# Where a recurrent kernel's bias enters PSUM, and three smaller moves around it

## The chip, the core and the metric

The kernel runs on one NeuronCore of a Trainium2 chip. The time is device microseconds of one launch; smaller is better. The core has five engines that run beside each other and meet only at semaphores: TensorE (PE, matrix products into PSUM), VectorE (DVE), ScalarE (ACT), GpSimd (POOL) and SyncE (SP, which here only issues DMAs; ACT issues a few too). Each engine works through its own instructions in order.

## The reference

The input is `x` of 16 batches, 512 time steps and 512 features, and one condition vector of 512 per batch. Four layers follow one another, each added to its input:

```python
x = x + L0(x, cond)   # levels of sums and differences, gated: comes to x * (1 + gate)
x = x + L1(x, cond)   # h = tanh(x_t @ Wx + b + h @ Wh), h0 = cond, over 512 steps
x = x + L2(x, cond)   # gated recurrence: sigmoids, cumulative sums along time
x = x + L3(x, cond)   # x @ (base + A_b B_b): A, B of rank 8, made from cond by a small network
```

All of it is float32. The bias of L1, `b`, is what this case is about: it is a vector of 512 that is added to each step's input before the tanh.

## The kernel before

**Start (lines 126 to 264).** DMAs bring the small vectors and weights in. `turned_layer` computes L0's gate from the condition in two layers of 16 matrix products (`ps_hq`, then `ps_g`); DVE turns and adds, ACT takes the sigmoid, and the gate plus 2 becomes `g2`. `gated` multiplies a block of the input by it (`x1`, four DVE instructions). Beside this the layer norm of the condition goes through four small PE transposes into `aeT`. The L1 bias is loaded by ACT's DMA queue into three rows of `rest`, split by POOL into three bfloat16 pieces whose sum is the float32 value, and kept in three rows of `bias_rows`. Last, the table `b2a` (8 numbers for each of 512 rows of L3's first factor) is loaded into `b2a_raw` by ACT's queue (line 229), transposed by PE (line 231) and copied by DVE (line 232) to `b2a_sb`. Only the last stage reads it.

**Recurrence (lines 446 to 525).** 64 blocks of `T = 8` steps. The order of PE, ACT, DVE and SP is written by hand here: instructions stand in each engine's queue as the Python code emits them. All batches go together. A PSUM tile `pre` of three banks holds the sums of one block; two generations of it (of bufs=2) are in use, one for the block that runs (`pre`) and one for the next (`nxt`). `PAIRS` and `PLACE` say that a place of 128 columns serves two steps: bank 0 has the pairs (0, 5) and (2, 7), bank 1 (4, 1), bank 2 (6, 3). In each step `s` of block `n`:

- PE adds 16 products of the last state with `wh_sb` (`accumulate`, line 465), waiting chunk by chunk for `h_out`;
- PE adds two of the 16 input pieces of the next block (`inputs`, line 475), each four products with `wx_sb`; when a piece is the first of its bank, the bias goes in before it: four bfloat16 products of `ones_rows` with `bias_rows` (line 354), which with `start=True` also open the bank. That falls on step 0 (bank 0, 256 columns), step 2 (bank 1, 128 columns) and step 6 (bank 2, 128 columns);
- from block 1 to 16, in steps 4 to 7, PE adds four products of L3's small network (`factor_part`; in block 0 the first layer of it);
- from block 16 on, in each step, PE computes a quarter of a unit of L2's gates for the first 128 times, eight products of 256 columns (`early_gate`, line 382). Three units make a group of 12 steps: f, i, candidate. Their sigmoids and the DVE work on them are laid into later steps by `later` and `do_jobs`;
- ACT takes four tanhs of 128x32 (line 491) and DVE four transposes of 128x32 into `h_out` (line 492), on which the next step's products wait; DVE then adds the states to `x2` or gates input of block n+2; then come the jobs of the step.

In block 0 the pieces of block 0 itself stand in steps 0 to 2 too, beside those of block 1. At the end of block 0 `finish_first` takes a Gelu on ACT, which needs a load of its table.

**Last stage (lines 527 to 629).** For each batch, four chunks `j` of L2 (`gate_unit`: 12 products of 384 columns on PE, two sigmoids on ACT, some 9 us of DVE, two adds on POOL, giving `x3[:, j]`). After chunk 2 `make_layer` forms L3's matrix: four products into PSUM tiles (two of tag `pl`, two of the tag `po` that the output also uses), and four DVE additions of `base_sb` spread among the next chunk's DVE work. `last_layer` of a batch stands after chunk 1 of the next one, in the last batch after chunk 3: 4 x 4 products of 512 columns into `po`, ACT copies, DMAs out. The last batch's matrix is written over `base_sb`.

Of the kernel before, what the change touches and what calls it, by code (L numbers as in the profile page):

```python
# [35 lines left out]
P = 128  # L36
# [4 lines left out]
T = 8  # L41
# [21 lines left out]
def kernel(  # L63
# [55 lines left out]


# [8 lines left out]
    nc.gpsimd.memset(hT3, 0.0)  # L129
    for h in h_out[G - 2 : T - 1]:  # L130
        nc.gpsimd.memset(h, 0.0)

    bias_rows = rw.tile([P, D], BF16)
    ones_rows = rw.tile([P, BP], BF16)
    thirds = [slice(i * BP, i * BP + 1) for i in range(3)]
    nc.gpsimd.memset(bias_rows, 0.0)
    nc.gpsimd.memset(ones_rows, 0.0)
    for rows in thirds:
        nc.gpsimd.memset(ones_rows[rows, :], 1.0)
# [36 lines left out]
    with tc.tile_pool(name="pre", bufs=1, side="right") as pre, tc.tile_pool(  # L176
# [36 lines left out]
        rest = pre.tile([P, D], F32)  # L213
        piece = pre.tile([P, D], BF16)
        nc.gpsimd.memset(rest, 0.0)
        for rows in thirds:
            nc.scalar.dma_start(
                out=rest[rows, :].rearrange("p (k n) -> p k n", k=KC),
                in_=l1b.rearrange("(o k) n -> o k n", o=1),
            )  # L220
        for i, rows in enumerate(thirds):
            nc.gpsimd.tensor_copy(piece, rest)
            nc.gpsimd.tensor_copy(bias_rows[rows, :], piece[rows, :])
            if i < 2:
                nc.gpsimd.tensor_tensor(rest, rest, piece, ALU.subtract)

        b2a_raw = pre.tile([P, KC, BP], F32)
        nc.gpsimd.memset(b2a_raw, 0.0)
        nc.scalar.dma_start(out=b2a_raw[:, :, :R], in_=b2a)
        ps = ps_pre.tile([P, P], F32, tag="ae", name="b2a_turned")  # L230
        nc.tensor.transpose(ps, b2a_raw.rearrange("p k r -> p (k r)"), ident)
        nc.vector.tensor_copy(b2a_sb, ps)
# [112 lines left out]
    def inputs(n, i, pre):  # L345

        g, k = divmod(i, KC)
        bank, place = PLACE[g]
        if k == 0 and place == 0:

            n_place = sum(b == bank for b, _ in PLACE)
            for j in range(KC):
                row = tile_columns(bias_rows, j).unsqueeze(1).to_broadcast([P, n_place, KC, BP])
                nc.tensor.matmul(  # L354
                    pre[bank][j * BP : (j + 1) * BP, :n_place, :],
                    ones_rows,
                    row,
                    start=True,
                    stop=False,
                    skip_group_check=True,  # L360
                )
# [80 lines left out]
    def fresh(n):  # L442
        return [ps_r.tile([P, G, P], F32, tag=f"pre{i}", name=f"pre_{n}_{i}") for i in range(NBANK)]
# [4 lines left out]
    pre = fresh(0)  # L448
# [3 lines left out]
    for n in range(NBLK):  # L452
        if n + 1 < NBLK:
            nxt = fresh(n + 1)
# [5 lines left out]
        for s in range(T):  # L460
# [12 lines left out]
            if n + 1 < NBLK:  # L473
                for i in range(2 * s, 2 * s + 2):
                    inputs(n + 1, i, nxt)
# [31 lines left out]
            do_jobs(q)  # L507
        if n == 0:
            finish_first(loaded)
        elif loaded:  # L510
            store_factor(n - 1, loaded)
# [10 lines left out]
        pre, loaded = nxt, coming  # L522
# [92 lines left out]
    for b in range(B):  # L615
# [72 lines left out]
```

## Time and profile before

| what | us |
|---|---|
| median of 3 runs (1676.74 to 1680.77) | 1678.63 |
| the profiled execution | 1677.59 |
| its span, first to last instruction | 1675.8 |
| first tanh of the recurrence starts | 25.45 |
| first tanh of block 1 starts | 41.95 |
| first products of the last stage | 925.64 |
| last product of PE ends | 1672.16 |

How busy the engines are in some stretches of that span, in us of busy time:

| stretch | length | PE | DVE | ACT | POOL |
|---|---|---|---|---|---|
| 56.80 to 255.00, blocks 2 to 15 and some | 198.20 | 192.17 | 97.60 | 56.55 | 0.00 |
| 270.00 to 910.00, blocks 17 to 61 and some | 640.00 | 638.00 | 371.47 | 192.58 | 0.00 |
| 925.60 to 1580.00, batches 0 to 13 of the last stage | 654.40 | 654.17 | 554.44 | 97.26 | 183.17 |
| 1635.10 to 1641.44 | 6.34 | 0.00 | 6.34 | 0.00 | 0.56 |

The lines of the trace are read as: start, duration, engine, line of the kernel, operation, what it writes and reads, shape, count, and in brackets the idle time of the engine before it and who ended it. A matrix product's duration includes its way through the array: 16 products of 128 columns in float32, which the trace counts as 32 instructions, follow each other 0.03 us apart although each lasts 0.27 us. So PE counts as busy while it waits for a short time; the start times tell more.

### The profile page before, as it was taken

What the parts mean: (1) busy time and instruction counts of PE and PEld (TensorE: products, weight loads), DVE (VectorE), ACT (ScalarE), POOL (GpSimd) and SP (SyncE); (2) the same over time, 40 slices, a digit from 0 to 9 for tenths busy, and PEclk for the clock granted to TensorE, in tenths of its full rate; (3) what the DMA queues carried; (4) which work ended last, traced back from release to release, by engine and by line L of the source; (5) the groups of instructions that cost most, each with busy time, mean ns of one, the idle gap of its engine ahead of it and who ended that gap; (6) DMA issues with size and microseconds to landing.
All of it is one profiled execution on the core that took longest, in us unless ns stands there. A gap on an engine that the chain in (4) does not pass through costs nothing.

```text
span 1675.8 us, 71396 instructions
## 1 busy us (share of the span) xinstructions
PE 1638.2 (98%) x31205; PEld 1196.9 (71%) x31205; DVE 1126.2 (67%) x3557; ACT 381.6 (23%) x2315; POOL 213.4 (13%) x223
## 2 busy tenths in 40 slices
PE   6999999999999999999999999999999999999997
PEld 5888889898898888999998555555555555555553
DVE  3444545555555555555555888889888888888894
ACT  2222232323323322333323111111111111111111
POOL 2000000000000000000000222232232323222231
PEclk9999999999999999999999999999999999999998
DMA  5344331111111111111110011110101111111101
GB/s 190 104 142 151 117 96 31 36 36 36 34 35 36 36 36 36 36 36 36 36 36 17 24 40 40 38 37 22 39 33 38 40 37 40 37 40 38 40 15 50
DMA packets 100239, 83.61 MB, mean 50 GB/s; under 512 B 10307, under 2 KB 78403, under 8 KB 99926
## 3 DMA queue, kind: packets, MB, share of 16 engines
q1 hardware_dynamic: 99392, 79.02, 15.2%
q8 instruction: 244, 4.00, 1.0%
q14 instruction: 69, 0.57, 0.1%
q10 hardware_dynamic: 534, 0.02, 0.0%
HBM read 53.32 MB, written 25.69 MB: 47 GB/s over the span
## 4 chain that ended last, share of the span: by engine, by line
PE 89%; DVE 6%; issue 2%; DMA 1%; ACT 1%; POOL 0%; ACTq 0%; SPq 0%; DVEq 0%; POOLq 0%
PE pre L336 40%; PE po L607 12%; PE pg L382 10%; PE pf L541 8%; PE pi L541 8%; PE pc L541 8%; DVE s L558 2%; PE pf L308 1%; PE pl L597 1%; DVE s L566 1%; PE pre L354 1%; DVE h_out L492 1%; DVE s L570 1%; ACT a L491 1%; DMA b2a_raw<-in_b2a_dram 0%
## 5 line engine op out<-in xcount | busy, mean ns | idle before, releaser
L336 PE MATMUL pre<-wh_sb,h_out 128*32 128x128 f32 x16384 | 563.1, 274 | 7.4 <-DVE h_out L492 1.4
L336 PEld LDWEIGHTS pre<-wh_sb,h_out 128*32 128x32 f32 x16384 | 462.1, 110 | 97.0 <-DVE h_out L492 71.1
L492 DVE STREAM_TRANSPOSE h_out<-a 128x32 f32<-128x32 f32 x2048 | 262.0, 185 | 364.1 <-ACT a L491 363.5
L491 ACT ACTIVATE a<-pre 128x32 f32<-128x32 f32 x2048 | 238.3, 202 | 627.0 <-PE pre L336 626.8
L336 PE MATMUL pre<-wx_sb,x 128*32 128x128 f32 x8192 | 336.9, 274 | 2.0 <-issue 1.4
L336 PEld LDWEIGHTS pre<-wx_sb,x 128*32 128x32 f32 x8192 | 245.4, 110 | 5.5 <-issue 4.6
L607 PE MATMUL po<-layer,x 128*128 128x512 f32 x480 | 211.5, 599 | 6.3 <-DVE base_sb L600 6.3
L541 PE MATMUL pf<-x,wf_sb 128*128 128x384 f32 x512 | 177.3, 489 | 1.0 <-DVE x L497 1.0
L607 PEld LDWEIGHTS po<-layer,x 128*128 128x128 f32 x480 | 92.2, 192 | 120.2 <-issue 108.8
L541 PE MATMUL pi<-x,wi_sb 128*128 128x384 f32 x512 | 175.6, 486 | 0.0
L541 PE MATMUL pc<-x,wc_sb 128*128 128x384 f32 x512 | 175.6, 486 | 0.0
L558 DVE RECIPROCAL s<-s 128x384 f32<-128x384 f32 x64 | 163.4, 2553 | 2.2
L541 PEld LDWEIGHTS pf<-x,wf_sb 128*128 128x128 f32 x512 | 95.9, 190 | 79.9 <-issue 18.1
L541 PEld LDWEIGHTS pc<-x,wc_sb 128*128 128x128 f32 x512 | 97.3, 190 | 67.8
L541 PEld LDWEIGHTS pi<-x,wi_sb 128*128 128x128 f32 x512 | 97.3, 190 | 67.8
L575 POOL TENSOR_TENSOR s<-s,f 128x512 f32<-128x512 f32 x64 | 87.5, 1367 | 388.8 <-DVE s L570 376.2
L497 DVE TENSOR_TENSOR x<-x,h_out 128x128 f32<-128x128 f32 x256 | 101.1, 395 | 37.5 <-PE pg L382 13.8
L530 POOL MEMSET zero<- 128x1 f32 x1 | 0.1, 100 | 913.7 <-DMA early<-ei 913.7
L557 DVE SCALAR_TENSOR_TENSOR s<-f,i 128x384 f32<-128x384 f32 x64 | 36.6, 572 | 101.7 <-ACT i L556 101.7
L556 ACT ACTIVATE f<-pf,vec_sb 128x384 f32<-128x384 f32 x64 | 37.3, 583 | 276.1 <-POOL s L575 117.3
L611 ACT COPY osb<-po 128x512 f32<-128x512 f32 x64 | 37.5, 586 | 273.7 <-PE po L607 159.5
L382 PE MATMUL pg<-x,wc_sb 128*32 128x256 f32 x1024 | 84.0, 379 | 0.0
(88 smaller groups left out, 1317.7 us busy)
## 6 DMA issues: line engine op xcount, KB each, us to landing
xb<-in_xT_dram SPq DMA_DIRECT2D x64, 256.0 KB
w<-in_l3w_dram SPq DMA_DIRECT2D x64, 256.0 KB
out_dram<-osb SPq DMA_DIRECT2D x64, 256.0 KB
early<-ef SPq DMA_DIRECT2D x32, 128.0 KB
early<-ei SPq DMA_DIRECT2D x32, 128.0 KB
f<-early SPq DMA_DIRECT2D x64, 64.0 KB
i<-early SPq DMA_DIRECT2D x64, 64.0 KB
w_sb<-in_w1T_dram SPq DMA_DIRECT2D x1, 1024.0 KB
```

The lines of the kernel that those rows point to most:

```text
L336: nc.tensor.matmul(pre[PLACE[g][0]][j * BP : (j + 1) * BP, PLACE[g][1], :], lhsT, tile_columns(w, j), start=False, stop=False, skip_group_ ...
L382: nc.tensor.matmul(ps[c * BP : (c + 1) * BP, :, :], w[:, k, j * P + c * BP : j * P + (c + 1) * BP], x2[:, k, pair, :TE], start=(k == 0), s ...
L491: nc.scalar.activation(a[:, at], pre[bank][:, place, at], AF.Tanh)
L492: nc.vector.transpose(turned[:, c, :], a[:, at])
L497: nc.vector.tensor_tensor(x2[:, :, :, at].rearrange("p k b t -> p k t b"), xs[n][:, :, t0 // 2, :, :], turned.rearrange("p k (t b) -> p k ...
L541: nc.tensor.matmul(p[:, TE:], w_sb[:, k, j * P : (j + 1) * P], x2[:, k, b, TE:], start=(k == 0), stop=(k == KC - 1),)
L556: nc.scalar.activation(gate[:, new], p[:, new], AF.Sigmoid, bias=col(bias, j))
L557: nc.vector.scalar_tensor_tensor(s[:, new], f[:, new], EPS, i[:, new], ALU.add, ALU.add)
L558: nc.vector.reciprocal(s[:, new], s[:, new])
L575: nc.gpsimd.tensor_tensor(s, s, f, ALU.add)
L607: nc.tensor.matmul(po, x3[:, k, at], layer[:, k, :], start=(k == 0), stop=(k == KC - 1))
L611: nc.scalar.copy(osb, po)
```

## The change

- **Bias.** `bias_sb`, a float32 tile that holds the bias broadcast over the partitions, is loaded by four DMAs of ACT's queue. A new `begin(n, i)` allots one bank of block `n` and lets ACT copy the bias into it; the products of `inputs` add to that. In the banks' first two generations (blocks 0 and 1) PE first writes zeros with 32 products of a zero tile and `ident`, with `start=True` on the first of each bank and quarter. The products of line 354, `bias_rows`, `ones_rows` and POOL's splitting go.
- **When.** Bank 0 of block n+2 is begun at the end of step 7 of block n, bank 1 of block n+1 after step 0, bank 2 after step 2, each after the jobs of the step. Blocks 0 and 1 are begun ahead of the loop.
- **b2a.** Its memset and DMA stay at the start (the DMA now directly behind those of the bias on ACT's queue); its PE transpose and DVE copy go to the end of block 2.
- **Inputs in block 0.** Block 1's 16 pieces, two in each step before, stand in steps 3 to 7 as 3, 4, 3, 3, 3.
- **Last batch.** `make_layer` of the last batch stands after chunk 1 instead of 2.

In the built program the layer norm's transposes also stand ahead of `ps_hq` on PE, and its DVE work ahead of `z_hq`. The issue of `b2a_raw` on ACT's queue waits for the first of the four bias DMAs, and the table load and square root of the layer norm stand behind it.

```diff
-    bias_rows = rw.tile([P, D], BF16)
-    ones_rows = rw.tile([P, BP], BF16)
...
+    bias_sb = rw.tile([P, KC, BP], F32)
...
+        for j in range(KC):
             nc.scalar.dma_start(
-                out=rest[rows, :].rearrange("p (k n) -> p k n", k=KC),
-                in_=l1b.rearrange("(o k) n -> o k n", o=1),
+                out=bias_sb[j * BP : (j + 1) * BP],
+                in_=l1b[:, j * BP : (j + 1) * BP]
+                .rearrange("(o c) f -> o c f", o=1)
+                .to_broadcast([BP, KC, BP]),
             )
-        for i, rows in enumerate(thirds):
-            nc.gpsimd.tensor_copy(piece, rest)
-            nc.gpsimd.tensor_copy(bias_rows[rows, :], piece[rows, :])
-            if i < 2:
-                nc.gpsimd.tensor_tensor(rest, rest, piece, ALU.subtract)
...
         nc.scalar.dma_start(out=b2a_raw[:, :, :R], in_=b2a)
-        ps = ps_pre.tile([P, P], F32, tag="ae", name="b2a_turned")
-        nc.tensor.transpose(ps, b2a_raw.rearrange("p k r -> p (k r)"), ident)
-        nc.vector.tensor_copy(b2a_sb, ps)
...
     def inputs(n, i, pre):
         g, k = divmod(i, KC)
-        bank, place = PLACE[g]
-        if k == 0 and place == 0:
-            n_place = sum(b == bank for b, _ in PLACE)
-            for j in range(KC):
-                row = tile_columns(bias_rows, j).unsqueeze(1).to_broadcast([P, n_place, KC, BP])
-                nc.tensor.matmul(
-                    pre[bank][j * BP : (j + 1) * BP, :n_place, :],
-                    ones_rows,
-                    row,
-                    start=True,
-                    stop=False,
-                    skip_group_check=True,
-                )
...
+    def begin(n, i):
+        bank = ps_r.tile([P, G, P], F32, tag=f"pre{i}", name=f"pre_{n}_{i}")
+        n_place = sum(b == i for b, _ in PLACE)
+        if n < 2:
+            for j in range(KC):
+                for place in range(n_place):
+                    nc.tensor.matmul(
+                        bank[j * BP : (j + 1) * BP, place, :],
+                        h0[:, 0, :BP],
+                        ident,
+                        start=(place == 0),
...
+        nc.scalar.copy(
+            bank[:, :n_place, :],
+            bias_sb.rearrange("p c f -> p (c f)").unsqueeze(1).to_broadcast([P, n_place, P]),
+        )
+        return bank
+    SHARE = ((0, 0), (0, 0), (0, 0), (0, 3), (3, 7), (7, 10), (10, 13), (13, 16))
+    BEGINS = {T - 1: 0, 0: 1, 2: 2}
...
-    pre = fresh(0)
+    pre = [begin(0, i) for i in range(NBANK)]
+    nxt = [begin(1, i) for i in range(NBANK)]
...
-                for i in range(2 * s, 2 * s + 2):
+                for i in range(*((2 * s, 2 * s + 2) if n else SHARE[s])):
                     inputs(n + 1, i, nxt)
...
             do_jobs(q)
+            if s in BEGINS:
+                if s < T - 1 and 0 < n < NBLK - 1:
+                    nxt.append(begin(n + 1, BEGINS[s]))
+                elif s == T - 1 and n + 2 < NBLK:
+                    ahead.append(begin(n + 2, BEGINS[s]))
...
+        if n == 2:
+            turned = ps_q.tile([P, P], F32, tag="pg", name="b2a_turned")
+            nc.tensor.transpose(turned, b2a_raw.rearrange("p k r -> p (k r)"), ident)
+            nc.vector.tensor_copy(b2a_sb, turned)
...
-            if j == 2:
+            if j == (1 if end else 2):
```

More of the change, by code (lines that the diff above doesn't have):

```diff
@@ L118 @@
     wh_sb = rw.tile([P, KC, D], F32)
+    b2a_raw = rw.tile([P, KC, BP], F32)
     h_out = [rw.tile([P, KC, HP], F32, name=f"h_out_{i}") for i in range(2 + G)]
@@ L129 @@
     nc.gpsimd.memset(hT3, 0.0)
+    nc.gpsimd.memset(b2a_raw, 0.0)
     for h in h_out[G - 2 : T - 1]:
         nc.gpsimd.memset(h, 0.0)
-    bias_rows = rw.tile([P, D], BF16)
-    ones_rows = rw.tile([P, BP], BF16)
[L135 to L139, printed above, removed]
+    bias_sb = rw.tile([P, KC, BP], F32)
     def load_x(n, pool=xpool):
@@ L211 @@
             )
[L213 to L216, printed above, removed]
+        for j in range(KC):
             nc.scalar.dma_start(
-                out=rest[rows, :].rearrange("p (k n) -> p k n", k=KC),
-                in_=l1b.rearrange("(o k) n -> o k n", o=1),
-            )
-        for i, rows in enumerate(thirds):
-            nc.gpsimd.tensor_copy(piece, rest)
-            nc.gpsimd.tensor_copy(bias_rows[rows, :], piece[rows, :])
-            if i < 2:
-                nc.gpsimd.tensor_tensor(rest, rest, piece, ALU.subtract)
-        b2a_raw = pre.tile([P, KC, BP], F32)
-        nc.gpsimd.memset(b2a_raw, 0.0)
+                out=bias_sb[j * BP : (j + 1) * BP],
+                in_=l1b[:, j * BP : (j + 1) * BP]
+                .rearrange("(o c) f -> o c f", o=1)
+                .to_broadcast([BP, KC, BP]),
+            )
         nc.scalar.dma_start(out=b2a_raw[:, :, :R], in_=b2a)
-        ps = ps_pre.tile([P, P], F32, tag="ae", name="b2a_turned")
-        nc.tensor.transpose(ps, b2a_raw.rearrange("p k r -> p (k r)"), ident)
-        nc.vector.tensor_copy(b2a_sb, ps)
         def turned_layer(src, w_sb, which, name):
@@ L440, in do_jobs @@
             job()
-    def fresh(n):
-        return [ps_r.tile([P, G, P], F32, tag=f"pre{i}", name=f"pre_{n}_{i}") for i in range(NBANK)]
+    def begin(n, i):
[9 more added lines that the diff above has]
+                        start=(place == 0),
+                        stop=False,
+                        skip_group_check=True,
+                    )
+        nc.scalar.copy(
+            bank[:, :n_place, :],
+            bias_sb.rearrange("p c f -> p (c f)").unsqueeze(1).to_broadcast([P, n_place, P]),
+        )
+        return bank
+    SHARE = ((0, 0), (0, 0), (0, 0), (0, 3), (3, 7), (7, 10), (10, 13), (13, 16))
+    BEGINS = {T - 1: 0, 0: 1, 2: 2}
     E = mybir.EngineType
     rnn.enter_context(tc.manual_schedule(engines={E.PE, E.Activation, E.DVE, E.SP}))
-    pre = fresh(0)
+    pre = [begin(0, i) for i in range(NBANK)]
+    nxt = [begin(1, i) for i in range(NBANK)]
     for i in range(KC):
@@ L452 @@
     for n in range(NBLK):
-        if n + 1 < NBLK:
-            nxt = fresh(n + 1)
+        ahead = []
         if n + 2 < NBLK:
@@ L521 @@
                 nc.vector.scalar_tensor_tensor(diag, ident, 2.0, diag, ALU.mult, ALU.add)
-        pre, loaded = nxt, coming
+        if n == 2:
+            turned = ps_q.tile([P, P], F32, tag="pg", name="b2a_turned")
+            nc.tensor.transpose(turned, b2a_raw.rearrange("p k r -> p (k r)"), ident)
+            nc.vector.tensor_copy(b2a_sb, turned)
+        pre, nxt, loaded = nxt, ahead, coming
     for q in sorted(jobs):
```

## The prediction

> **What bounds the kernel now.** I read the page's busy times and chain of waits first, to see which engine carries the end, and then the timeline at four places where the change acts.
>
> ```profile
> PE 1638.2 (98%) x31205; PEld 1196.9 (71%) x31205; DVE 1126.2 (67%) x3557; ACT 381.6 (23%) x2315; POOL 213.4 (13%) x223
> ...
> PE pre L336 40%; PE po L607 12%; PE pg L382 10%; PE pf L541 8%; PE pi L541 8%; PE pc L541 8%; DVE s L558 2%; PE pf L308 1%; PE pl L597 1%; DVE s L566 1%; PE pre L354 1%; DVE h_out L492 1%; DVE s L570 1%; ACT a L491 1%; DMA b2a_raw<-in_b2a_dram 0%
> ```
>
> PE is busy 98% and nearly all of the chain is PE. The products of the bias (L354) hold 1%. Whether removing them pays must be read step by step, since a PE that waits inside a running product counts as busy. First, steps of block 1 (timeline; the tanh marks a step):
>
> ```profile
> 45.17 0.24 PE L354 MATMUL pre<-bias_rows,ones_rows 128*32 128x128 bf16 x4
> ...
> 45.42 0.47 ACT L491 ACTIVATE a<-pre 128x32 f32<-128x32 f32 x4 [1.05 <-PE pre L336]
> ...
> 47.06 0.47 ACT L491 ACTIVATE a<-pre 128x32 f32<-128x32 f32 x4 [1.18 <-PE pre L336]
> ...
> 48.71 0.47 ACT L491 ACTIVATE a<-pre 128x32 f32<-128x32 f32 x4 [1.18 <-PE pre L336]
> ```
>
> From tanh to tanh 1.64 and 1.65 us, the first with four bias products in it, the second without. Here the loop tanh, transpose, 16 products, tanh sets the step, and PE has room: the products of the state take 0.89 (45.92 to 46.81) and the pieces 0.45. A step of block 33 with the gates' products in it:
>
> ```profile
> 484.64 0.29 PE L354 MATMUL pre<-bias_rows,ones_rows 128*32 128x256 bf16 x4
> 484.89 0.47 ACT L491 ACTIVATE a<-pre 128x32 f32<-128x32 f32 x4 [1.28 <-PE pre L336]
> ...
> 486.75 0.47 ACT L491 ACTIVATE a<-pre 128x32 f32<-128x32 f32 x4 [1.39 <-PE pre L336]
> ...
> 488.49 0.47 ACT L491 ACTIVATE a<-pre 128x32 f32<-128x32 f32 x4 [0.92 <-PE pre L336]
> ```
>
> With the 256-column bias the step takes 1.86, the next, without, 1.74, the same as for many steps of this region; the 128-column ones give 1.79 to 1.80. Here PE is the bound: state 0.87, pieces 0.43, gates 0.44. Third, the start:
>
> ```profile
> 10.48 1.72 DVE L249 TENSOR_TENSOR z_hq<-z_hq,vec_sb 128x128 f32<-128x128 f32 x1
> ...
> 12.30 0.62 ACTq L229 DMA_DIRECT2D b2a_raw<-in_b2a_dram  x1
> ...
> 16.27 0.31 ACT L251 ACTIVATE gate_g<-z_g 128x128 f32<-128x128 f32 x1 [3.73 <-DVE z_g L249]
> ...
> 20.07 0.45 PE L231 MATMUL b2a_turned<-ident,b2a_raw 128*128 128x128 f32 x1 [4.55 <-DMA b2a_raw<-in_b2a_dram]
> 20.56 0.29 DVE L232 COPY b2a_sb<-b2a_turned 128x128 f32<-128x128 f32 x1 [4.33 <-PE b2a_turned L231]
> 20.77 0.18 DVE L258 TENSOR_SCALAR g<-gate_g 128x64 f32<-128x64 f32 x1
> ...
> 21.74 1.93 PE L336 MATMUL pre<-wx_sb,x 128*32 128x128 f32 x32 [0.43 <-DVE x L162]
> ```
>
> PE, DVE and so the first pieces of the recurrence (21.74) stood behind the landing of `b2a_raw` at about 20.0, although the gate was done at 16.58. Fourth, the last batch:
>
> ```profile
> 1632.36 2.74 PE L541 MATMUL pc<-x,wc_sb 128*128 128x384 f32 x8
> ...
> 1640.73 1.26 DVE L600 TENSOR_TENSOR base_sb<-pl,base_sb 128x512 f32<-128x512 f32 x2
> ...
> 1641.44 16.98 PE L607 MATMUL po<-layer,x 128*128 128x512 f32 x32 [6.34 <-DVE base_sb L600]
> ...
> 1652.66 1.27 POOL L576 TENSOR_TENSOR x<-s,x 128x512 f32<-128x512 f32 x1
> ```
>
> PE has nothing to do from 1635.10 to 1641.44: the output of batch 14 needs PSUM tiles that the last two additions to `base_sb` release, and these stand late in DVE's queue. The first 16 products then take 16.98 instead of 13.73, the time of every earlier batch.
>
> **What the Trainium skill says.** "PSUM — Partial Sum Buffer", The four PSUM rules: writes of VectorE and ScalarE neither set nor clear the bits by which a product decides to add or to overwrite. So zeros by PE are needed once for each buffer, and later generations can be seeded by ACT; no run here shows it. "TensorE: Matmul & The Clock Gate", Part 1: PE runs at half rate until it was busy for a window of about 3.4 us, and again after an idle one. The trace agrees: 32 instructions take 1.48 from 21.74 and 0.88 from 27.01, and weight loads take 0.34 instead of 0.19 after the gap at 1635. "SBUF — State Buffer", SBUF: two separate sides: a DVE instruction with two SBUF inputs and a GpSimd one that reads SBUF exclude each other. The trace agrees: the addition to `z_hq` at 10.48 took 1.72, beside POOL's bias work, its twin at 15.94 took 0.29.
>
> **Step 1, the start.** `ps_hq` begins with the landing of w1 at 8.14, as before; the four bias DMAs and the earlier b2a put about a thousand small packets ahead, 0.2 assumed (0 to 0.8). `z_hq` is done at 10.13 + 0.32 + 0.29 = 10.8 instead of 12.2; sigmoid 0.31, product 0.34, `ps_g` 1.94 end at 13.45; turn, add, sigmoid, `g2` 1.2 more: 14.7; three of the gatings of DVE 0.75: 15.5. But PE now has the 32 zero products: 64 instructions at the slow rate (1.48 for 32) are 2.95, from 13.5 or 13.9, so it reaches the first piece at 16.7, with the 0.2 at 16.9. `wx_sb` is there by my count of the packets (3.4 MB moved by 13.3). ACT's six copies overlap with the zeros. On SP the issues of x0, `wh_sb` and the first `l3w` chunk now wait for bias DMAs; with 2 MB of w1 and w2 queued ahead that costs nothing. Against 21.74 that is 4.8 earlier. PE then also gets its full rate sooner: continuous work from 13.9, and before it needed 5.1 (20.9 to 26.0), so 19.0; of the 4.3 us at half rate after the first piece some 2.1 remain, a gain of 1.1.
>
> **Step 2, block 0.** Steps 0 to 2 lose block 1's pieces and the bias: 0.87 + 0.87 = 1.74 each instead of 2.79, 2.18, 2.30; of that 2.05 the clock, counted above, is some 0.5. Steps 4 to 7 get them back: step 4 has 4 pieces and `factor_part`, 0.87 + 0.22 + 0.87 = 1.96 against 1.71; steps 5 and 6 1.74 against 1.65; step 3 stays at 1.64 (three pieces 0.65 fit beside the loop's 0.77). At the end ACT has a copy of 0.4 ahead of its 1.28 table load and the Gelus, with the next tanh behind: 0.4 lost. Sum 1.5 - 0.25 - 0.2 - 0.4 = 0.7, with 0.2 open on either side. Steps 1 and 2 together: 4.8 + 1.1 + 0.7 = 6.6 gained (4 to 8).
>
> **Step 3, the bias in the recurrence.** In blocks 1 to 15 it gives nothing: the steps keep 1.64, the copies of ACT fall into its idle 1.18 before each tanh. In blocks 16 to 62 each block loses 0.11 + 0.055 + 0.055 = 0.22 of PE: 47 x 0.22 = 10.3 gained. A step of 1.74 stays above the loop's 1.64, so nothing else is late next.
>
> **Step 4, ACT's copies.** No row shows an ACT write of SBUF to PSUM. The copy of 128x512 the other way (L611) takes 0.59; 0.37 to 0.40 for 256 columns (the skill's "ScalarE: Activation LUTs", What ACT_TABLE_LOAD costs, gives 0.186 + 0.83 ns a column: 0.40). Counted from the start of a step's tanhs (+), it is over at + 0.8 in steps 0 and 2, and nothing waits. In step 7 it is over at + 0.9, and the next block's first piece, behind the 16 products of step 0, comes at + 1.49. But the copy stands behind the step's jobs. The sigmoid of the input gate falls on steps 12g + 7 of the early gates, on step 7 of a block when g is even: 16 blocks. There:
>
> ```profile
> 511.46 0.47 ACT L491 ACTIVATE a<-pre 128x32 f32<-128x32 f32 x4 [1.33 <-PE pre L336]
> ...
> 512.33 0.47 ACT L407 ACTIVATE ei<-pg,vec_sb 128x256 f32<-128x256 f32 x1 [0.40 <-PE pg L382]
> ...
> 512.95 0.29 PE L354 MATMUL pre<-bias_rows,ones_rows 128*32 128x256 bf16 x4
> ...
> 513.20 0.47 ACT L491 ACTIVATE a<-pre 128x32 f32<-128x32 f32 x4 [0.40 <-PE pre L336]
> ```
>
> The sigmoid waits for the gates' products, 512.33 to 512.80, that is + 1.34. The copy ends between + 1.65 (overlapped as the four tanhs are, 0.09 apart) and + 1.78, and PE, in order, stands before the first piece from + 1.49 (+ 1.40 in the later blocks): 0.2 to 0.35, 0.27 taken; behind it wait the gates' products and the next step's. 16 x 0.27 = 4.3 lost (2 to 7). The tanh of the step is ready at + 1.74, so ACT is just free.
>
> **Step 5, b2a in block 2.** A PE transpose of some 0.1 and a DVE copy of 0.29 stand in the room of a 1.64 step: nothing, at most 0.2. If they weren't covered they would cost 0.4.
>
> **Step 6, the last batch.** The DVE additions move one chunk (9.1 us) up, to about 1624.7 to 1633, so the `po` tiles are free when PE ends its gates at 1635.10. DVE, without a gap since 1592, has the same work in total, so `x3`'s last chunk still comes from POOL at 1652.66 + 1.27 = 1653.93. PE does batch 14 in 13.73 to 1648.83, then three of the four k of the first tile, 2.57, to 1651.4, and is late next on `x3`: 2.5 us. From 1654.2 the rest takes 0.86 + 10.3 + 0.25, so the last copy starts at 1665.6 instead of 1672.24: 6.6 gained. The idle 2.5 may halve the clock again: before, 2.0 us of idle in a window did (half rate from 1637.1), 0.98 at 924.65 didn't. A throttled window costs 1.5 to 3.2; I take 1.5. Gain 5.1 (3.4 to 6.6).
>
> **Sum.** 6.6 + 10.3 - 4.3 + 5.1 = 17.7. The profiled execution, 1677.59 (span 1675.8 and 1.8 around it), comes to 1659.9; it lies 1.0 under the median of the runs shown, so 1660.9 on that scale. I give 1660.7.
>
> **Rivals.** *ACT is held at the start* (14%). The issue of `b2a_raw` waits for the first bias DMA, and the layer norm's table load and square root stand behind it; the transposes that need them now stand ahead of `ps_hq`. If the bias lands as late as `rest` did (4.80 after its issue, at 9.5), then 0.6 + 1.28 + 0.2 + 0.15 + 0.53 + a transpose put `ps_hq` at 12.5: 4.3 lost, 1665.0. Against it: the bias DMAs go out at about 0.7 to 2.3, before w1's packets fill the engines. *ACT gets away with the copies and the clock holds* (18%): step 4 costs 1 and the tail keeps 6.6: 1655.9. *Slower: the copies are slow* (4%). If ACT's write with a broadcast source took over 1.24, each copy would end after tanh + 0.5 + 1.24 and delay the next tanh, on the loop in all 64 blocks, three in each: it eats the 22 that the rest gives from a delay of 0.115 on, a copy of about 1.36. At 1.6 (four times L611's rate) it is 190 x 0.36 = 68 lost less 22: 1725. The rate of L611 speaks against it. *The change doesn't do what it says* (2%): PE waits in every step 0 for ACT by 0.3, 14 lost more, and the start is held: near 1679.
>
> **How the numbers follow.** The main case has 62%: 1660.7, its own range 1657 to 1665. The cases either side stretch it to 1654.5 and 1666.5. A difference under 0.2%, 3.4 us, can't be told from none: faster 0.94 (main, both milder cases), same 0.02, slower 0.04.
>
> **What would show it.** Right: first piece of the recurrence at about 17; steps 0, 2 and 6 of late blocks at 1.74; in 16 blocks, every third, PE idle ahead of the first piece until the copy ends; PE going from gates to output without a gap at the end, and one of 2.5 within the last batch. Wrong: a start at over 20, a copy over 0.6, steps of block 1 to 15 off 1.64, or additions to `base_sb` that still end after PE's gates.

## The result, and the profile after

The changed kernel takes 1657.33 us (median of 4 runs, 1656.52 to 1659.06), the kernel before 1677.68 (4 runs, 1673.54 to 1680.77): 0.9882 of the time, 95% interval 0.9858 to 0.9905. That is 20.3 us less where 17.7 were forecast. Measured once more, the changed kernel took 1655.83 (4 runs) against 1676.69 (7 runs): 0.9879, 0.9862 to 0.9895.

The profiled execution took 1657.68, its span is 1655.8. Line numbers below are those of the kernel that is read: in the changed one the products of state and inputs are L320, the tanh L485, its transpose L486, ACT's bias copy L428, the zero products L420, the gates L352 and L377, the output L610. First the page of the changed kernel (busy times, and the chain by line), then one line of its list of waits (who waits, for whom, us in total, times, longest):

```profile
PE 1627.2 (98%) x30501; PEld 1176.0 (71%) x30501; DVE 1125.6 (68%) x3557; ACT 426.4 (26%) x2507; POOL 207.0 (12%) x209
...
PE pre L320 40%; PE po L610 12%; PE pg L352 10%; PE pf L544 9%; PE pi L544 9%; PE pc L544 9%; DVE h_out L486 1%; DVE s L561 1%; PE pl L600 1%; ACT a L485 1%; PE pf L292 1%; DVE s L569 0%; DMA w_sb<-in_w1T_dram 0%; DVE s L573 0%; DVE i L572 0%
```

```profile
PEld pre L320 <- ACT pre L428: 4.2, 16, 0.3
```

The bias has left PE's line of the chain and turned up on ACT, 426.4 us busy instead of 381.6. PE is as full as before, and waits for the new copies 16 times, 4.2 us in all.

Where the 19.9 us between the two profiled executions are, by start times of the same instructions:

| stretch | before | after | difference |
|---|---|---|---|
| span's start to the first tanh | 25.45 | 20.53 | -4.92 |
| block 0 | 16.51 | 17.06 | +0.55 |
| blocks 1 to 16 | 216.42 | 216.04 | -0.38 |
| blocks 17 to 62 | 654.41 | 645.65 | -8.76 |
| last stage, to the gates of the last chunk | 706.72 | 705.41 | -1.31 |
| from there to PE's last product | 39.80 | 34.76 | -5.04 |

**The recurrence.** Four steps of a late block, ACT alone in the timeline; then the step in which the copy is late, all engines:

```profile
484.98 0.47 ACT L485 ACTIVATE a<-pre 128x32 f32<-128x32 f32 x4 [0.40 <-PE pre L320]
486.73 0.47 ACT L485 ACTIVATE a<-pre 128x32 f32<-128x32 f32 x4 [1.28 <-PE pre L320]
488.47 0.47 ACT L485 ACTIVATE a<-pre 128x32 f32<-128x32 f32 x4 [1.27 <-PE pre L320]
490.21 0.47 ACT L485 ACTIVATE a<-pre 128x32 f32<-128x32 f32 x4 [1.28 <-PE pre L320]
490.70 0.38 ACT L428 COPY pre<-bias_sb 128x256 f32<-128x256 f32 x1
```

```profile
293.89 0.47 ACT L485 ACTIVATE a<-pre 128x32 f32<-128x32 f32 x4 [1.28 <-PE pre L320]
...
294.76 0.47 ACT L377 ACTIVATE ei<-pg,vec_sb 128x256 f32<-128x256 f32 x1 [0.40 <-PE pg L352]
295.13 0.38 ACT L428 COPY pre<-bias_sb 128x256 f32<-128x256 f32 x1
295.56 0.38 PEld L320 LDWEIGHTS pre<-wx_sb,x 128*32 128x32 f32 x16 [0.26 <-ACT pre L428]
...
295.63 0.47 ACT L485 ACTIVATE a<-pre 128x32 f32<-128x32 f32 x4
```

Nearly all steps take 1.74 or 1.75 now, whether a bank is begun in them or not (before, 1.85 or 1.86 and 1.80 where the bias products stood); the medians of the eight steps add up to 13.93 instead of 14.15. A copy of 256 columns takes 0.38. Where no sigmoid stands ahead of it, it begins 0.49 after the tanhs and nobody waits. In the second listing the step began at 293.89, the copy stands behind the sigmoid of the input gate, and PE's weight load waits 0.26 for it, until + 1.67 (counted from the step's first tanh). The step that follows takes 1.95 from tanh to tanh: in blocks 17, 20, ... 62, 16 times 0.2 more. Besides these, four single steps of this execution are 0.16 to 0.9 longer.

**The start**, where `gate_g` is done at 15.56 instead of 16.58:

```profile
8.11 0.60 PE L223 MATMUL ps_hq<-w_sb,h_out 128*32 128x128 f32 x2 [1.79 <-DMA w_sb<-in_w1T_dram]
...
9.44 0.18 PEld L204 LDWEIGHTS ae<-ident,xhat 16*128 16x128 f32 x1 [0.38 <-DVE aeT L205]
...
9.66 1.50 PE L223 MATMUL ps_hq<-w_sb,h_out 128*32 128x128 f32 x22
...
11.57 0.29 DVE L233 TENSOR_TENSOR z_hq<-z_hq,vec_sb 128x128 f32<-128x128 f32 x1
...
14.95 3.67 PE L420 MATMUL pre<-ident,h_out 128*32 128x128 f32 x64 [0.44 <-DVE z_g L232]
...
18.36 1.17 PE L320 MATMUL pre<-wx_sb,x 128*32 128x128 f32 x32
...
20.53 0.47 ACT L485 ACTIVATE a<-pre 128x32 f32<-128x32 f32 x4 [1.60 <-PE pre L320]
```

Nothing waits for `b2a_raw` any more, and the addition to `z_hq` takes 0.29 where it took 1.72 beside POOL's bias work. But `ps_hq` needs until 11.16: only two of the layer norm's four transposes stand ahead of it, and the other two stand among its products (after 2 and after 10 of the 32 instructions), the second of them waiting 0.38 for DVE. The zero products come at 14.95, behind the turning of `z_g`, and the first input piece behind them, at 18.36.

**The last batch**, PE, POOL and DVE in the timeline:

```profile
1633.86 2.74 PE L610 MATMUL po<-base_sb,x 128*128 128x512 f32 x6
...
1635.24 1.20 DVE L573 TENSOR_TENSOR_SCAN s<-i,zero 128x512 f32<-128x512 f32 x1
1636.53 1.26 POOL L578 TENSOR_TENSOR s<-s,f 128x512 f32<-128x512 f32 x1 [6.30 <-DVE s L573]
1637.86 1.26 POOL L579 TENSOR_TENSOR x<-s,x 128x512 f32<-128x512 f32 x1
...
1639.18 13.12 PE L610 MATMUL po<-base_sb,x 128*128 128x512 f32 x26 [2.58 <-POOL x L579]
...
1640.37 0.34 PEld L610 LDWEIGHTS po<-base_sb,x 128*128 128x128 f32 x1 [0.47 <-issue]
```

The gap of 6.34 ahead of the output is gone. One of 2.58 is left, in the output itself, and what ends it is the last chunk of `x3` from POOL. From 1639.9 to 1643.3 the weight loads take 0.34 instead of 0.19: the granted clock, as the trace records it, is halved for 3.41 us.

### The profile page after: what moved, and what is told of

Same layout as the page of the kernel before. It is cut to its first block, busy times and chain, and to the rows that moved or that the text cites. A ratio compares the mean times of both kernels' runs of the same rounds, so it can differ in the third digit from the quotient of the medians.

```text
span 1655.8 us, 70230 instructions
## 1 busy us (share of the span) xinstructions
PE 1627.2 (98%) x30501; PEld 1176.0 (71%) x30501; DVE 1125.6 (68%) x3557; ACT 426.4 (26%) x2507; POOL 207.0 (12%) x209
## 4 chain that ended last, share of the span: by engine, by line
PE 93%; DVE 4%; issue 1%; ACT 1%; DMA 0%; SPq 0%; POOLq 0%; POOL 0%; DVEq 0%; ACTq 0%
PE pre L320 40%; PE po L610 12%; PE pg L352 10%; PE pf L544 9%; PE pi L544 9%; PE pc L544 9%; DVE h_out L486 1%; DVE s L561 1%; PE pl L600 1%; ACT a L485 1%; PE pf L292 1%; DVE s L569 0%; DMA w_sb<-in_w1T_dram 0%; DVE s L573 0%; DVE i L572 0%
## 5 line engine op out<-in xcount | busy, mean ns | idle before, releaser
L320 PE MATMUL pre<-wh_sb,h_out 128*32 128x128 f32 x16384 | 547.6, 273 | 10.2 <-DVE h_out L486 1.5
L320 PEld LDWEIGHTS pre<-wh_sb,h_out 128*32 128x32 f32 x16384 | 454.7, 109 | 107.4 <-DVE h_out L486 101.8
L486 DVE STREAM_TRANSPOSE h_out<-a 128x32 f32<-128x32 f32 x2048 | 262.1, 185 | 359.4 <-ACT a L485 358.4
L485 ACT ACTIVATE a<-pre 128x32 f32<-128x32 f32 x2048 | 238.2, 202 | 566.9 <-PE pre L320 564.9
L320 PE MATMUL pre<-wx_sb,x 128*32 128x128 f32 x8192 | 320.9, 273 | 1.3 <-issue 1.2
L320 PEld LDWEIGHTS pre<-wx_sb,x 128*32 128x32 f32 x8192 | 235.6, 110 | 6.9 <-ACT pre L428 4.2
L610 PE MATMUL po<-layer,x 128*128 128x512 f32 x480 | 208.4, 592 | 0.0
L610 PEld LDWEIGHTS po<-layer,x 128*128 128x128 f32 x480 | 91.2, 190 | 111.6 <-issue 107.6
L579 POOL TENSOR_TENSOR x<-s,x 128x512 f32<-128x512 f32 x64 | 81.4, 1272 | 5.0
```

What stands on the lines that cost most here:

```text
L320: nc.tensor.matmul(pre[PLACE[g][0]][j * BP : (j + 1) * BP, PLACE[g][1], :], lhsT, tile_columns(w, j), start=False, stop=False, skip_group_ ...
L485: nc.scalar.activation(a[:, at], pre[bank][:, place, at], AF.Tanh)
L486: nc.vector.transpose(turned[:, c, :], a[:, at])
L579: nc.gpsimd.tensor_tensor(x3[:, j, :], s, x2[:, j, b, :], ALU.add)
L610: nc.tensor.matmul(po, x3[:, k, at], layer[:, k, :], start=(k == 0), stop=(k == KC - 1))
```

## The experiments

Times in us. "17 to 62" and the like are blocks, from the first tanh of one to the first of the next; "tail" is from the gates of the last chunk to PE's last product. All but the last column come from one profiled execution each.

| kernel | first piece | first tanh | block 0 | 1 to 15 | 17 to 62 | tail | time |
|---|---|---|---|---|---|---|---|
| before | 21.74 | 25.45 | 16.51 | 201.21 | 654.41 | 39.80 | 1677.68 |
| changed | 18.36 | 20.53 | 17.06 | 201.00 | 645.65 | 34.76 | 1657.33 |
| last batch only | 21.45 | 25.16 | 17.54 | 204.54 | 652.59 | 33.08 | 1673.43 |
| b2a only | 17.54 | 20.81 | 17.02 | 203.41 | 652.56 | 38.69 | 1672.71 |
| bias only | 20.66 | 22.72 | 18.55 | 200.36 | 644.88 | 39.91 | 1665.09 |
| even share | 17.79 | 19.85 | 19.34 | 202.65 | 645.00 | 34.78 | 1660.25 |
| copy first | 17.27 | 19.33 | 18.06 | 202.37 | 641.35 | 33.07 | 1652.88 |
| two copies | 17.63 | 19.68 | 18.47 | 201.68 | 650.96 | 33.06 | 1662.69 |
| cheap zeros | 17.16 | 20.92 | 16.48 | 201.20 | 644.61 | 33.08 | 1654.91 |
| norm later | 17.18 | 19.53 | 17.54 | 202.58 | 645.96 | 33.07 | 1657.33 |
| both edits | 16.45 | 18.50 | 17.79 | 201.21 | 641.95 | 33.05 | 1652.58 |
| changed again | 17.39 | 19.46 | 18.32 | 201.60 | 644.34 | 33.07 | 1655.83 |
| no loads | 16.30 | 18.37 | 17.84 | 198.45 | 641.82 | 33.08 | 1648.68 |
| spread loads | 17.48 | 19.83 | 17.30 | 201.73 | 641.61 | 34.76 | 1655.07 |

The first four experiments had one run each, beside one of the kernel before of 1673.8, the next four beside one of 1675.47; the last three rows and "both edits" have 2 to 4 runs, beside 1676.69 for the kernel before ("both edits", "changed again") and 1679.65 (the last two rows). The totals of different groups come from different chips and aren't compared directly. With single runs the stretches are compared, not the totals, because blocks 0 to 16 differ by some us between executions of whatever kernel.

**One part alone: the last batch.** The kernel before with:

```diff
-            if j == 2:
+            if j == (1 if end else 2):
```

> The kernel before, with only the last batch's matrix one chunk sooner. Theory (late additions on VectorE hold the PSUM tiles): the 6.34 us gap of TensorE before the output of batch 14 goes, one of about 2.5 us before the last chunk's products of batch 15 comes, with one half-rate window of 3.4 us; from the start of the last candidate products to the end of TensorE 39.8 us become about 34.8; the whole time falls by 5.0 us. Rival (VectorE is the bound there anyway and sets the end): the end moves by less than 1.5 us.

PE's gap went from 6.34 to 2.61, ended by POOL as in the changed kernel, and the tail from 39.80 to 33.08: 6.7 less, without a halved clock this time. In all eleven executions with this edit the tail is either 33.05 to 33.08, or, in three, 34.76 to 34.78 with 3.41 us of halved clock: throttling costs 1.7. The total fell by only 0.4 where 5.0 were forecast. Blocks 0 to 15 of this execution took 4.4 more than in the first trace of before, which would hide the gain; the run of before beside it has no trace, so that isn't shown.

**One part alone: b2a.** The kernel before, its transpose and copy of `b2a` put to the end of block 2 (the same lines as in the change), nothing else.

> The kernel before, with only b2a turned over at the end of block 2. Theory (the landing of b2a_raw held g2 and with it the start): the first input piece moves from 21.74 to about 17.6 us, the first tanh from 25.45 to about 21.3, the time by -4.1 us; the loop is unchanged at 1.85, 1.74 and 1.80 us for its steps. Rival (GpSimd's splitting of the bias or the loads hold the start): the first piece stays later than 20 us.

The first piece stands where the theory put it, and waits for the gating alone. Timeline of this kernel:

```profile
15.98 0.40 PE L351 MATMUL pre<-bias_rows,ones_rows 128*32 128x256 bf16 x4 [0.50 <-POOL bias_rows L224]
...
16.79 0.90 DVE L163 TENSOR_TENSOR x<-xb,g 128x128 f32<-128x128 f32 x4
17.54 1.48 PEld L333 LDWEIGHTS pre<-wx_sb,x 128*32 128x32 f32 x32 [1.45 <-DVE x L163]
```

So the landing of `b2a_raw` alone was worth 4.2 at the first piece and 4.64 at the first tanh. POOL's pieces of the bias are waited for by 0.50, in an interval in which DVE isn't ready either. The total fell by 1.1 where 4.1 were forecast: blocks 0 to 15 took 2.7 more than in the first trace of before, and again the run beside it has no trace.

**One part alone: the bias.** The changed kernel with the rest put back:

```diff
-                for i in range(*((2 * s, 2 * s + 2) if n else SHARE[s])):
+                for i in range(2 * s, 2 * s + 2):
...
-        if n == 2:
-            turned = ps_q.tile([P, P], F32, tag="pg", name="b2a_turned")
...
-            if j == (1 if end else 2):
+            if j == 2:
```

and the transpose of `b2a` again at the start.

> The kernel before, with only the bias through ScalarE (b2a turned at the start, inputs of block 1 even, last batch as before); the b2a load stands behind the bias loads on ScalarE's queue, ahead of its table load. Theory: in late blocks steps 0, 2 and 6 take 1.74 us and 16 waits of 0.26 us for the copy come, together -6.9 us; at the start b2a lands early because its load is issued at 2.9 us instead of 12.3, so it no longer holds anything and the first piece stands near 18.5 us; in all -9 to -10.5 us. Rival (turning b2a later is what frees the start): the first piece comes after 21.7 us or, with the 3.2 us of zero products behind b2a, near 25; in all about -4 us.

The loop does what was expected: steps of 1.74, sixteen of 1.94, 644.88 for blocks 17 to 62. The start lies between the two theories, at 20.66. The early DMA lets `b2a_raw` land at 11.6 instead of 20, but the transpose now stands in PE's queue among the products of `ps_hq`:

```profile
11.64 0.45 PE L218 MATMUL b2a_turned<-ident,b2a_raw 128*128 128x128 f32 x1 [1.64 <-DMA b2a_raw<-in_b2a_dram]
...
12.02 0.87 PE L226 MATMUL ps_hq<-w_sb,h_out 128*32 128x128 f32 x12
```

PE waits 1.64 for it there, and the zero products, which start at half rate in all these traces, begin at 17.31, against 14.95 and 14.98 in the two traces of the changed kernel. The move to block 2 is thus worth some 2.3 also beside an earlier load. The total fell by 8.7, a little under the 9 to 10.5 of the forecast.

**The share of block 0.** The changed kernel with `range(2 * s, 2 * s + 2)` for all blocks.

> The changed kernel, with block 1's inputs two pieces in each step of block 0 again. Theory (TensorE is the bound in steps 0 to 2 of block 0): these steps take 2.18 instead of 1.74 us, steps 4 to 7 get 0.7 us back, so from the first tanh to the first of block 1 +0.6 us. Rival (the late inputs were worth nothing, since stops of TensorE with nothing to wait for are larger than that): no difference, or one of either sign that comes with such stops.

Block 0 took 2.3 longer, but two stops of PE (0.94 and 1.77) lie in it. Of the steps without a stop, step 2 took 2.18 where it took 1.75 with the late share (the kernel with cheap zeros), and step 4 1.71 instead of 1.96: the pattern that was expected. By the time alone the run decides nothing.

**The copy ahead of the sigmoid.** Bank 0 is begun behind the tanh of step 7, before the jobs of the step, and no longer behind them:

```diff
+            if s == T - 1 and n + 2 < NBLK:
+                ahead.append(begin(n + 2, BEGINS[s]))
             do_jobs(q)
-            if s in BEGINS:
-                if s < T - 1 and 0 < n < NBLK - 1:
-                    nxt.append(begin(n + 1, BEGINS[s]))
-                elif s == T - 1 and n + 2 < NBLK:
-                    ahead.append(begin(n + 2, BEGINS[s]))
+            if s in BEGINS and s < T - 1 and 0 < n < NBLK - 1:
+                nxt.append(begin(n + 1, BEGINS[s]))
```

> The changed kernel, with the copy of step 7 ahead of the step's jobs on ScalarE instead of behind them. Theory (the copy is late only because the input gate's sigmoid stands ahead of it and waits for TensorE): the 16 waits of 0.26 us of the first input piece for the copy go, step 0 of every third late block falls from 1.95 to 1.74 us, the median block stays at 13.93; -3.4 us over blocks 17 to 62. The sigmoid still starts with the gates' products, since the copy ends at 0.9 us after the start of the tanhs. Rival (ScalarE's write into PSUM is slow to reach TensorE, wherever it stands): the steps stay near 1.95 us.

```profile
294.85 0.47 ACT L485 ACTIVATE a<-pre 128x32 f32<-128x32 f32 x4 [1.28 <-PE pre L320]
...
295.35 0.38 ACT L428 COPY pre<-bias_sb 128x256 f32<-128x256 f32 x1
...
295.72 0.47 ACT L377 ACTIVATE ei<-pg,vec_sb 128x256 f32<-128x256 f32 x1
296.24 0.48 PEld L320 LDWEIGHTS pre<-wx_sb,x 128*32 128x32 f32 x16
...
296.60 0.47 ACT L485 ACTIVATE a<-pre 128x32 f32<-128x32 f32 x4 [0.40 <-PE pre L320]
```

In the same step as above the copy now ends at + 0.88, the sigmoid starts as far from its step's tanh as before, and PE's load of the first piece carries no wait. The waits for the copy are gone from the list, all steps of 1.95 are 1.74, and the stretch takes 641.35, that is 3.0 to 4.3 less than the 644.3 to 645.7 of the two traces of the changed kernel.

**Two copies.** Where bank 0 is begun, ACT copies twice (`for _ in range(2 if i == 0 and n > 1 else 1)`), to see whether the wait follows the copy.

> The changed kernel, with the copy of bank 0 made twice from block 2 on. Theory (the copy's end behind the sigmoid sets the wait): in every third late block step 0 grows by the second copy, 0.29 to 0.38 us, to 2.24 to 2.33 us; the other blocks keep 1.74 us, since two copies still end before the first piece at 1.49 us after the start of the tanhs. The tanhs of step 0 in those blocks also wait, so the step before may take 0.1 to 0.3 longer. Rival (the wait is a fixed delay of the semaphore or of TensorE's queue): steps stay at 1.95 us.

```profile
PEld pre L320 <- ACT pre L429: 10.7, 16, 0.7
```

The same 16 places wait, now 0.7 each, with steps of 2.13 behind them and 1.96 in the step ahead; all others but two stay at 1.74. The step with the wait was forecast at 2.24 to 2.33; about half of the second copy shows in the step ahead instead. One more copy costs nothing where there is no sigmoid, and 0.40 (0.61 instead of 0.21) where there is.

**Cheaper zeros.** Four bfloat16 products of a zero tile for each bank instead of one float32 product for each place.

> The changed kernel, with the 32 float32 zero products (64 instructions, 3.2 us from 14.95) replaced by 24 bfloat16 products of zeros, 128 or 256 columns each, some 1.3 us. Theory (the zero products hold the first piece): it moves from 18.36 to about 16.7, where the gated input is ready, -1.6 us, the first tanh by -1 to -1.6 us. Rival (the half-rate clock eats it, since TensorE is busy for a shorter time before the first piece): the first tanh moves by less than 0.5 us.

```profile
15.04 1.04 PE L421 MATMUL pre<-zero_rows 128*32 128x256 bf16 x24 [0.44 <-DVE z_g L234]
...
17.16 1.94 PE L322 MATMUL pre<-wx_sb,x 128*32 128x128 f32 x32 [1.08 <-ACT pre L429]
...
20.92 0.47 ACT L486 ACTIVATE a<-pre 128x32 f32<-128x32 f32 x4 [3.76 <-PE pre L322]
```

The rival was right in that the first tanh didn't come sooner. The zeros take 1.04 and the first piece stands at 17.16, but a piece takes 1.94 instead of 1.17: PE gets its full rate at 22.3 instead of 18.6. It had less to do ahead of the piece, and it also stood idle for 1.08 between the zeros and the piece, waiting for ACT's copy of the bias; which of the two kept the rate down was not tried. The first tanh of this one execution is 0.4 later than in the first trace of the changed kernel, and 1.5 later than in the second.

**The layer norm later.** Its transposes and `aeT` are written behind `gate_hq` instead of ahead of `ps_hq`.

> The changed kernel, with the layer norm's transposes emitted behind the first gate layer, so that three of the four stand behind the 16 products of ps_hq instead of among them. Theory (the transposes among ps_hq, with their waits for VectorE, made it end at 11.16 instead of 10.07): z_hq is turned at about 10.1, the first piece comes at about 17.3 instead of 18.36 us (give or take 0.6 for the clock), the first tanh by about -1 us. Rival (the loads are the limit, or the transposes hold ps_g instead): no move of the zero products' start at 14.95.

```profile
9.98 0.32 DVE L226 STREAM_TRANSPOSE z_hq<-ps_hq 128x128 f32<-128x128 f32 x1 [3.41 <-PE ps_hq L217]
...
11.40 1.93 PE L217 MATMUL ps_g<-w_sb,hq 128*32 128x128 f32 x32 [0.59 <-DVE hq L234]
```

`z_hq` is turned at 9.98 instead of 11.21, and the first tanh comes at 19.53, 1.0 earlier than in the first trace of the changed kernel. The second trace stands at 19.46 without the edit, with its full rate from 16.3 instead of 18.6; so by the first tanh the comparison with that one says nothing. The start of the zero products, ahead of any full rate, shows the gain without the clock: they begin at 13.77, against 14.95 and 14.98 in the two traces of the changed kernel. The next pair, with full rates 0.6 apart, shows what is left of it at the first tanh.

**Both edits, and the changed kernel again.** The two edits above, the copy first and the layer norm later, in one kernel, five rounds each on one chip.

> The changed kernel with two edits together: the bias of block n + 2's pieces is copied after step 7's tanh instead of after step 6's, behind which no piece waits, and the LayerNorm's transposes stand behind gate_hq on PE instead of among the products of ps_hq. If the two gains add (3.4 us from sixteen steps of 1.95 that go back to 1.74, 1.0 us from the first tanh at 19.5 instead of 20.5), it takes about 1653 us where the changed kernel takes 1657, 0.985 to 0.987 of the kernel before, with 641 to 642 us for blocks 17 to 62 and a first tanh at 19.5. Rival: what is gained at the start is lost in the stops of PE in blocks 0 to 16, or the first tanh is set by the clock as with the cheap zeros; then it takes 1654 to 1656 us, and the first tanh stands at 20.3 or later or blocks 0 to 16 take more than 235 us.

> The changed kernel once more, on the same chip as the kernel with the two edits: 1656 to 1659 us, 0.987 to 0.990 of the kernel before, first tanh at 20.5, sixteen steps of 1.95 in blocks 17 to 62. If the stops of PE in blocks 0 to 16 are what differs from execution to execution, only the stretch between the first tanh and block 17 differs from the first trace by more than 0.5 us, the last batch apart.

With both edits 1652.58 (1651.21 to 1653.64), 0.9859 of before (0.9844 to 0.9874), against 1655.83 for the changed kernel: 3.3 less. 2.4 of that shows in blocks 17 to 62, where the sixteen waits are worth 3.3 and the version with both edits happened to have 0.9 more in single longer steps, and 0.96 in the first tanh (18.50 and 19.46), with full rates from 15.8 and 16.3. Both first tanhs came about 1.0 sooner than expected. The changed kernel's own second trace differs from its first by 1.07 at the first tanh and by 1.3 in blocks 17 to 62, so the expectation that only blocks 0 to 16 differ missed.

**Where the stops come from.** In blocks 0 to 16 PE stands at times with nothing that it waits for; the profile calls the releaser "issue". The single DMA packets of the traces point to queue 8, which by its count carries PE's instructions. On the page of the changed kernel:

```profile
q8 instruction: 239, 3.92, 1.0%
```

239 packets for 61002 instructions of PE (30501 loads, 30501 products) are 255 each; the kernel before has 244 for 62410, the one with cheap zeros 238 for 60922, both 256 each. In all 14 traces I took every weight load from the first tanh to the end of block 16 that carries no wait and starts over 0.3 us behind the end of the load before, and the last packet of queue 8 that had landed by then. There are 84 such stops, and all 84 end 1.20 to 1.62 us after such a landing, though packets come only every 4 us or so. They also stand at fixed places among PE's instructions, a packet apart: in the changed kernel and its variants ("bias only" and "cheap zeros" aside) PE stopped after its instruction 9638, loads and products counted, wherever the 37th packet was the last that had landed (five traces), and after 12958 where it was the 50th (four). Some of the stops, from the two traces of the changed kernel:

```
kernel          load starts   stop   after the packet's landing
changed              25.36    0.75   1.28
changed              62.71    0.39   1.30
changed             100.60    0.87   1.28
changed             170.46    1.01   1.34
changed, again       21.12    1.32   1.49
changed, again       25.95    1.29   1.33
changed, again      104.50    0.72   1.25
changed, again      199.88    0.76   1.40
```

So such a stop is an instruction packet that came late. The stops also go with the time that blocks 1 to 15 take: the two longest, 203.41 and 204.54, hold 5.0 and 5.4 us of them, the other eleven with the same loads 1.9 to 3.3. Two runs ask why a packet is late. The first takes the loads of the small network's weights away, from the version with both edits:

```diff
-        load_chunks(w, l3w2[which, r], f"w2_{i}", ks)
+        w.extend(wh_sb[:, k, :] for k in ks)
```

> The version with the two edits, but L3's small network takes its second weights from the resident wh_sb instead of the 64 chunks of 256 KB that are loaded in blocks 0 to 15: those loads are left out, and the factors are computed from the wrong weights; the products, the other DMAs and all else stay. It asks where the stops of PE in blocks 0 to 16 come from. Theory: PE's own instructions come by DMA in packets of 256 (queue 8 of the page: 239 packets for 61002 instructions), and a stop is a packet that came late because 300 to 800 KB of data had just been queued ahead of it. Then blocks 1 to 15 take 198 to 199.5 us instead of the 200.4 to 204.5 of the runs so far (120 steps of 1.644 are 197.3), no stop of over 0.3 us is left in them but those where a chunk of xb or of the last stage's weights was just issued, and the stretch loses its spread. Rival: the stops have nothing to do with the loads; then the blocks take 200.4 or more as before.

Blocks 1 to 15 took 198.45 instead of 201.21, with not one such stop in them; a single one is left, in block 0. All 13 other traces lie between 200.36 and 204.54. The loads are the cause of most of what lies between 201.2 and the 197.3 of 120 steps of 1.644: 2.8 of 3.9. The second spreads them:

```diff
-            if n < 2 * R and s in (1, KC + 2):
-                coming = load_factor(n, coming, range(KC // 2) if s == 1 else range(KC // 2, KC))
+            if n < 2 * R and s in (0, 2, 5, 7):
+                k = (0, 2, 5, 7).index(s)
+                coming = load_factor(n, coming, range(k, k + 1))
```

> The version with the two edits, and the four chunks of 256 KB of the small network's weights are issued one at a time, behind steps 0, 2, 5 and 7, instead of two and two behind steps 1 and 6; nothing is left out. If a late instruction packet is what stops PE, at most 256 KB stand ahead of one instead of 512 and more: the stops get shorter than the margin PE has, blocks 1 to 15 take 198.5 to 200.5 us instead of 201.2, and the median lies 0.5 to 2.5 us under the 1652.6 of the version with the two edits. Rival: as many packets are late as before, only each by less or at other places; then the stretch takes 200.5 to 202 and the median stays within 1 us of 1652.6.

The rival was right for the stretch, 201.73. The whole took 1655.07, more than 1 us off the 1652.6 that the rival named, but on a chip on which the kernel before is 3.0 slower too: 0.9857 of before (0.9833 to 0.9880), no better than the 0.9859 of the version with both edits. That packets are late beside these loads is shown; that the size of the burst ahead of one decides is not.

## Why the prediction was right

The forecast of 1660.7 lies 3.4 over the measured 1657.33. That the sum came so near is in part luck: the start gave 2.2 less than its steps forecast, and 3.2 came from stops of PE in blocks 17 to 62 and from the last stage, which stand in no step. By the prediction's own steps, profiled execution against profiled execution:

- **Steps 1 and 2, 6.6 forecast, 4.4 measured** (4.92 less 0.55). The mechanism of step 1 is as told: no wait for `b2a_raw`, the addition beside POOL back at 0.29, the first piece behind the zeros. It was mis-sized. The first piece was put at 16.9 and came at 18.36, since `ps_hq` was priced as before while two of the layer norm's transposes now stand among its products (1.1), and the zeros took 3.21 from 14.95 instead of 2.95 from 13.5 or 13.9. Full rate was forecast for 19.0 and came at 18.6 and 16.3. In step 2 the block as a whole lost 0.55 where 0.7 were to be gained. Its single time steps are right where PE has no stop: 1.72 for time step 1, 1.64, 1.96 and 1.75 for 3, 4 and 6, as told, and 2.99 for the last, which has the 0.40 of the copy ahead of the table load. Only time step 5 isn't: 2.13 for 1.74 in all these kernels but "bias only" (1.72), its transposes beginning 0.71 after the tanh instead of 0.30, for a reason that no run shows. The stops of PE (0.75 and 0.38 in this execution) were not in the sum.
- **Step 3, 10.3 forecast.** 14.15 less 13.93 is 0.22 a block, as told; in 46 blocks 10.1. Block 16 gave 0.17, blocks 1 to 15 nothing that exceeds their noise.
- **Step 4, 4.3 lost forecast, 3.4 measured.** 16 waits of 0.26 where 0.27 were taken; 0.05 of each is caught up before the next tanh, so 16 x 0.21. The two runs with an earlier copy and a double one show that the copy behind the sigmoid is the cause. Of the 8.76 in blocks 17 to 62, 6.7 is thereby explained; the other 2.0 lies in single longer steps, nearly all with a stop of PE in them: 3.2 in this execution of before and 1.3 in this one of the changed kernel (before's 654.41 stand against 652.6 in two other traces with the same steps).
- **Step 5, 0 forecast (at most 0.2), 0.28 measured.** The last step of block 2 takes 1.92 or 1.93 instead of 1.64 in each kernel with `b2a` there, stops apart. This step of the prediction failed where it let the room of a 1.64 step hide a transpose. Timeline of the changed kernel's second execution:

```profile
62.65 0.49 DVE L486 STREAM_TRANSPOSE h_out<-a 128x32 f32<-128x32 f32 x4 [0.73 <-ACT a L485]
...
62.94 0.33 PE L523 MATMUL b2a_turned<-ident,b2a_raw 128*128 128x128 f32 x1
...
63.20 1.08 PE L320 MATMUL pre<-wh_sb,h_out 128*32 128x128 f32 x32
```

  The state's first chunk is ready about when the transpose starts, and its products stand behind it in PE's queue: 0.26 of the transpose lies on the loop, outside the room that PE has.
- **Step 6, 5.1 forecast, 5.04 measured**, with its parts: a gap of 2.5 (2.58), a throttled window of 1.5 (1.7). The window comes by chance: three of eleven executions had it, so against this trace of before the gain is 6.7 more often than 5.0 (the tails of the three kernels without the edit are 38.69 to 39.91). The prediction read before's half rate from 1637.1; it begins at 1637.24, 2.1 after the start of the gap.
- **Not in the sum:** 1.31 in the last stage ahead of the last chunk. It is there in every kernel whose bias comes from ACT (705.41 or 705.42) and in none that has the bias products (706.56 to 706.72). It lies in batch 1 alone (45.96 instead of 47.11 to 47.27), where the first outputs go to memory: SP issues three of their DMAs in 3.18 instead of 5.15, and the copies behind them end sooner. The cause wasn't tried and stays open.

Of the rivals, "ACT is held at the start" fell: the transposes that need ACT's square root were done before `ps_hq` ended, though their place cost 1.1. "ACT gets away with the copies" fell in its first half, with 16 waits, and holds in its second in eight executions of eleven. The slow copy fell: 0.38, where it needed 1.36. So did the wait in every step 0: it comes in 16 blocks of 46.

The Trainium skill's rule that was carried over unproven ("PSUM — Partial Sum Buffer", The four PSUM rules) is borne out by this case in the half that the change needs, that ACT's writes don't clear the bits: of 192 banks that ACT seeds with the bias, 186 have no opening product, and PE's products add to what stands there, so that the sums have the bias in them. By "TensorE: Matmul & The Clock Gate", Part 1, PE falls back to half rate after an idle window of about 3.4 us. Here the measurement differs and decides: gaps of up to 1.76 us never halved the clock, one of 2.6 did in three of eleven executions, for 3.41 us, so a length of idle time alone doesn't decide it.

## What to carry to other kernels

A constant that each accumulation starts from can be written into PSUM by an engine with time to spare, and what it costs is read from its place in that engine's queue: here the copies were free in all steps but the last of block 0, where one stands ahead of a table load, and those in which a sigmoid that waits for PE stands ahead of them. One changed order brought the latter back (3.3 us together with a second small edit). Work that nobody needs before the end should not stand at the start in the queue of the engine that bounds the kernel, whether its data comes early or late: on both kernels it held the products behind it. A shorter stretch on PE ahead of a chain isn't a gain if PE is at half rate in the chain for longer, as the one trace with the cheap zeros shows; count both before trimming it.

## What the runs showed that was not expected

- PE's instructions themselves arrive by DMA, in packets of about 255, and PE stands still for 0.3 to 1.8 us where one is late: all 84 stops found end 1.2 to 1.6 us after a landing. Blocks 1 to 15 lose 2.8 us of 201 beside the small network's loads, going by the one trace without them, and the stops go with the spread of these blocks, 200.4 to 204.5 from execution to execution.
- The same kernel had its first tanh at 20.53 and 19.46, with full rate from 18.6 and 16.3, the same instructions ahead of it and the zero products begun at 14.95 and 14.98: when the clock steps up is alone worth about 1.0 at the start.
- With the zero products at the start 2.6 us shorter (1.04 instead of 3.67) the first tanh came 0.4 to 1.5 later, in the one execution that was traced; how it comes out in others isn't shown.
